# The last but one GRU step's chain in halves of the width, with accumulators of its own for z and for the transposes

## The chip, the cores and the metric

The kernel runs on one core of one Trainium2 chip. A core has TensorE (matrix products[...]), VectorE and ScalarE (elementwise work, both can read PSUM), GpSimd (POOL) and SyncE, which here only starts transfers. The metric is the device time of one execution in microseconds, lower is better.

## The reference

Two layers are computed in float32 on an input x of 128 sequences, 64 steps and a width of 512. The first layer runs a GRU over the steps, projects its states with a ternary weight, and adds the result to x:

```python
def cell(h, x):
    gi = x @ W_ih + b_ih
    gh = h @ W_hh + b_hh
    i_r, i_z, i_n = jnp.split(gi, 3, axis=-1)
    h_r, h_z, h_n = jnp.split(gh, 3, axis=-1)
    r = jax.nn.sigmoid(i_r + h_r)
    z = jax.nn.sigmoid(i_z + h_z)
    n = jnp.tanh(i_n + r * h_n)
    h_new = (1.0 - z) * n + z * h
    return (h_new, h_new)
...
x = x + _L0_ffn_ref(_L0_cond_ref(cond_2048, x, ...), L0_ffn_weight, L0_ffn_bias)
x = x + _L1_ffn_ref(_L1_cond_ref(x, cond_2048[:, None, :], L1_cond_b), ...)
```

The second layer is a causal convolution over the 128 sequences (channel by channel, with `cond_2048` as its taps), and then a mixture of 64 experts of which each token uses 6, with a shared expert beside them. Each GRU step needs the state of the step before; this is what the change is about.

## The kernel before

**Tiles and stages.** The batch of 128 lies on the 128 partitions and the width of 512 along them. The GRU comes first (0 to about 1407 us), then the convolution in 16 slices of the width (to about 1467), then the gating with the first half of the shared expert, then the experts.

**A GRU step.** The loop over `t` (L554) makes, for each of the gates r, n and z in this order, four products of the turned state `hT` with a block of `whh` into an accumulator of 128x512 (`psgh0`, `psgh2`, `psgh1`, L580 to L586). In float32 each product is two records in the profile. VectorE then adds the input part `gi` to r (L590), ScalarE applies the sigmoid (L591); n goes through three VectorE instructions (bias L602, times r L603, plus `gi` L604) and a tanh (L605); z takes one addition (L607) and a sigmoid (L608). The new state is `(h - n) * z + n`, three VectorE instructions (L611, L612, L613). `transposed` (L464) turns it: four 128x128 transposes on TensorE into one accumulator `psf` (`turned_up`, L461), and one copy by ScalarE to `hT` (L467). `parts` (L470) splits `hT` into two pieces, `hhi` and `hlo`, for the projection.

**What lies over the chain.** Inside a step, `ffn(t - 1, ...)` (L478) projects the state of the step before: eight products into `psf` (L490), then VectorE makes `x1` from it (L501), and SyncE stores `x1` twice, once as `x1c` for the convolution (L503) and once to the output (L513). And `stream`, a generator (L430 to L456), gives out the input products of later steps piece by piece (L399, 256 columns wide, into `psx`, `psy`, `psw`, `psz`), ten or eleven pieces a step (L617), so that TensorE has work while VectorE and ScalarE finish a state. The stream has its last pieces in step 61 and none in step 62.

**After the loop.** Three groups of the convolution's first slice go into `psx`, `psy` and `psw` (L626), then the last state's transposes, the fourth group into `psz`, and the last projection. The convolution's slices live in four pairs of buffers, `xc` (inputs, read back from `x1c`) and `tz` (taps); a slice's loads wait until TensorE has finished the slice that used its buffer before. The first two slices' last 16 steps, and slices 2 and 3 whole, are loaded by SyncE right behind the stores of step 61's `x1` (L507 to L511). `psc` rotates over four accumulators; VectorE adds each group to `hid` (L691). `tail_products` (L658) is a little extra work on `xl` and `tap` there.

**What sets the order.** The program is written in one order, and a scheduler reorders the instructions of each engine from it and puts in the semaphores; `tc.issue_after(i)` keeps an instruction behind another one. Each engine works through its own list in order.

## Time and profile before

| what | value |
|---|---|
| median of three runs | 2647.52 us (2647.27, 2647.52, 2649.79) |
| the profiled execution's own time | 2647.67 us |
| its span, first to last instruction | 2645.9 us |
| TensorE busy | 2631.8 us, 99% of the span |
| VectorE, ScalarE, POOL busy | 1402.9, 427.4, 453.2 us |
| TensorE's share of the chain that ended last | 98% |
| granted TensorE clock | 1.00 |

A row of the profile that tells of a group of instructions has the line, the engine, the operation, what it writes and reads, the shape and the count; then the group's busy time, the mean of one in ns, and how long its engine had been idle before it and on whom it waited. A row of the timeline has the start and the length in us first. The chain of waits is followed back from the last instruction, always to what released the one before; "issue" in it is time in which an engine waited for nothing that the profile shows. TensorE's records overlap each other, so that the distance between their starts says more than their length.

### The profile page before, as it was taken

The page shows a single profiled execution, that of the slowest core. Times are in us where ns is not written, and L with a number is a line of the kernel's source. Part 1 is how long each engine was busy: PE and PEld are TensorE (multiplying, and loading weights), DVE is VectorE, ACT ScalarE, POOL GpSimd, SP SyncE. Part 2 cuts the span into 40 slices and gives each one's busy share as a digit, 9 for nine tenths or more (in the row PEclk, how much of TensorE's full clock was granted, in tenths as well). Part 3 has the DMA queues.
Part 4 walks back from the last instruction along what each step waited for, and adds up shares of the span by engine and source line. Part 5 has one row for each costly group of instructions (what it writes and reads, how often), then busy time and mean ns, then how long its engine had stood idle before and what let it go on. Part 6 is the DMA issues. An engine that isn't in the chain of part 4 may idle for free.

```text
span 2645.9 us, 31136 instructions
## 1 busy us (share of the span) xinstructions
PE 2631.8 (99%) x11985; PEld 1823.5 (69%) x11985; DVE 1402.9 (53%) x3103; ACT 427.4 (16%) x791; POOL 453.2 (17%) x516
## 2 busy tenths in 40 slices
PE   9999999999999999999999999999999999999999
PEld 7666666666666666666668767788886666666667
DVE  6555555555555555555557755666674433433344
ACT  1111111111111111111110222222321111111111
POOL 2112111111112121111114100000002222222210
PEclk9999999999999999999999999999999999999999
DMA  5333233232322222322228911222356999998952
GB/s 197 74 58 66 56 60 61 53 61 53 61 47 52 44 52 44 76 44 52 44 60 293 332 41 26 40 66 66 82 148 185 283 313 278 302 326 271 297 174 48
DMA packets 476276, 323.33 MB, mean 122 GB/s; under 512 B 329056, under 2 KB 396512, under 8 KB 473952
## 3 DMA queue, kind: packets, MB, share of 16 engines
q1 hardware_dynamic: 447536, 248.18, 33.7%
q0 software_dynamic: 28592, 73.16, 11.4%
q8 instruction: 95, 1.56, 0.2%
q14 instruction: 53, 0.43, 0.1%
HBM read 235.01 MB, written 92.55 MB: 124 GB/s over the span
## 4 chain that ended last, share of the span: by engine, by line
PE 98%; DVE 1%; DMA 1%; issue 0%; SPq 0%; ACT 0%; DVEq 0%
PE psgh L583 25%; PE psz L787 7%; PE psw L787 7%; PE psx L787 7%; PE psz L399 6%; PE psw L399 6%; PE psx L399 6%; PE psf L490 4%; PE y L787 4%; PE py L1502 3%; PE psy L399 3%; PE pg L1476 3%; PE pu L1476 3%; PE y L962 2%; PE psc L182 2%; PE psf L461 1%
## 5 line engine op out<-in xcount | busy, mean ns | idle before, releaser
L583 PE MATMUL psgh<-whh,hT 128*128 128x512 f32 x1536 | 674.5, 595 | 0.7 <-ACT hT L467 0.7
L583 PEld LDWEIGHTS psgh<-whh,hT 128*128 128x128 f32 x1536 | 286.8, 190 | 350.7 <-issue 336.5
L399 PE MATMUL psx<-wih,xp 128*128 128x256 f32 x744 | 191.0, 379 | 0.0
L220 POOL DMA_DIRECT2D xn<-in_x_dram x61 | 33.8, 555 | 840.6 <-DVE x L501 828.2
L399 PEld LDWEIGHTS psx<-wih,xp 128*128 128x128 f32 x744 | 139.0, 190 | 18.0 <-issue 0.5
L1485 DVE SCALAR_TENSOR_TENSOR a<-a,rw,pu 128x352 f32<-128x352 f32 x32 | 18.6, 580 | 220.3 <-PE pu L1476 220.3
L602 DVE TENSOR_TENSOR n<-psgh,bhn 128x512 f32<-128x512 f32 x64 | 44.2, 691 | 171.0 <-PE psgh L583 171.0
L467 ACT COPY hT<-psf 128x512 f32<-128x512 f32 x64 | 37.5, 587 | 559.0 <-PE psf L461 558.9
L590 DVE TENSOR_TENSOR r<-psgh,gi 128x512 f32<-128x512 f32 x64 | 44.2, 691 | 141.7 <-PE psgh L583 141.7
L1064 POOL DMA_DIRECT2D out_dram<-hid x32 | 27.6, 1000 | 451.8 <-issue 332.9
L486 POOL TENSOR_TENSOR xn<-xn,fb 128x512 f32<-128x512 f32 x61 | 77.0, 1262 | 144.4 <-DMA xn<-in_x_dram 144.4
L399 PE MATMUL psz<-wih,xs 128*128 128x256 f32 x372 | 95.6, 379 | 0.1
L399 PE MATMUL psy<-t,xs 128*128 128x256 f32 x372 | 95.5, 379 | 0.0
L399 PE MATMUL psw<-t,xp 128*128 128x256 f32 x372 | 95.5, 379 | 0.0
L399 PE MATMUL psz<-t,xs 128*128 128x256 f32 x372 | 95.5, 379 | 0.0
L399 PE MATMUL psw<-wih,xp 128*128 128x256 f32 x372 | 95.4, 379 | 0.0
L490 PE MATMUL psf<-sgn,hhi 128*128 128x512 f32 x256 | 94.9, 492 | 0.3 <-DVE hlo L475 0.3
L1502 PE MATMUL py<-wd,aeT 128*64 128x512 f32 (+1 forms) x384 | 89.5, 601 | 0.0
L605 ACT ACTIVATE n<-n 128x512 f32<-128x512 f32 x64 | 40.3, 629 | 277.2 <-DVE n L604 277.2
L414 DVE TENSOR_TENSOR p<-psx,bi 128x512 f32<-128x512 f32 x93 | 64.3, 691 | 36.7 <-PE psx L399 36.7
L787 PE MATMUL psx<-xr,swg 128*128 128x256 f32 x320 | 83.3, 383 | 0.0
L787 PE MATMUL psx<-hid,swg 128*128 128x256 f32 x320 | 82.4, 380 | 0.0
(323 smaller groups left out, 4747.7 us busy)
## 6 DMA issues: line engine op xcount, KB each, us to landing
wg<-in_w_gate_dram SPq DMA_DIRECT2D x64, 704.0 KB
wu<-in_w_up_dram SPq DMA_DIRECT2D x64, 704.0 KB
wd<-in_w_down_dram SPq DMA_DIRECT2D x64, 512.0 KB
x1c<-x SPq DMA_DIRECT2D x62, 256.0 KB
out_dram<-x SPq DMA_DIRECT2D x62, 256.0 KB
xn<-in_x_dram POOLq DMA_DIRECT2D x61, 256.0 KB, 4.1
xp<-in_xT_dram POOLq DMA_DIRECT2D x30, 512.0 KB, 5.7
xc<-x1c SPq DMA_DIRECT2D x28, 512.0 KB
```

Of the source, the lines that this page charges most:

```text
L182: i = nc.tensor.matmul(ps[rows, j].rearrange("p h (u t) -> p h u t", u=2), xcs[sl % NCB][:, rows, g * 4 + j], tzs[sl % NCB][:, :, :, g * 4 ...
L399: i = nc.tensor.matmul(ps, self.ops[n][:, k, :], self.ws[n][:, k, :], start=(first and k == 0), stop=(k == HK - 1), skip_group_check=not f ...
L414: add(self.p1, both, b)
L486: nc.gpsimd.tensor_add(xn, xn, fb)
L490: nc.tensor.matmul(ps, piece[:, k, :], sgn[:, k, :], start=(i == 0 and k == 0), stop=(i == 1 and k == KD - 1),)
L583: nc.tensor.matmul(ps, hT[:, k, :], whh[c][:, k, :], start=(k == 0), stop=(k == KD - 1))
L590: i = nc.vector.tensor_add(r, ps_r, gis.pop((t, 0)))
L602: nc.vector.tensor_add(n, ps_n, bhn)
L787: i = nc.tensor.matmul(ps.rearrange("p (j b) -> p j b", b=P) if len(r.shape) == 3 else ps, lhs(k), r, start=(first and k == 0), stop=(k == ...
L962: nc.tensor.matmul(gu.rearrange("p (j b) -> p j b", b=P), swr[:, k].rearrange("p w n -> p (w n)"), rows[:, k], start=(k == 0), stop=(k == ...
L1476: nc.tensor.matmul(acc[halves[j]], self.xeT[:, k, halves[j]], self.ws[j][which][:, k, :], start=(k == 0), stop=(k == KD - 1),)
L1502: nc.tensor.matmul(py[halves[j]], self.aeT[:n, c, halves[j]], self.ws[j][2][:n, c, :], start=(c == 0), stop=(c == len(ech) - 1),)
```

## The change

In step 62 (`t == T - 2`) and nowhere else the work behind the n gate is done in two halves of 256 columns:

- z's products are made in halves, into two accumulators taken from the pool of the input products, `psx` for the left half and `psy` for the right one.
- The instructions on n, then those on z and on the new state, run once for each half.
- The transposes go into `psw` instead of `psf`, and ScalarE's copy to `hT` becomes two copies.
- `x1` of step 61, which is made in the same step, is ordered behind the last instruction of the new state.

In all other steps the instructions are those of before; the loops have one turn there. Beyond step 62 the scheduler's lists differ in one place: in `tail_products`, the second multiplication on `xl` stands right behind the first, and eight of VectorE's additions to `hid` follow it that stood between the two.

```diff
-        def turned_up(src):
-            ps = ps_f.tile([P, D], F32, name="psf").rearrange("p (k b) -> p k b", k=KD)
+        def turned_up(src, ps=None):
+            if ps is None:
+                ps = ps_f.tile([P, D], F32, name="psf")
+            ps = ps.rearrange("p (k b) -> p k b", k=KD)
...
-        def transposed(src):
-            ps = turned_up(src)
+        def transposed(src, by=1):
+            ps = turned_up(src, ps_gi.tile([P, D], F32, name="psw") if by == 2 else None)
             hT = el0.tile([P, KD, B], F32, name="hT")
-            nc.scalar.copy(hT, ps)
+            for n in range(by):
+                part = slice(n * KD // by, (n + 1) * KD // by)
+                nc.scalar.copy(hT[:, part], ps[:, part])
             return hT
...
-            nc.vector.scalar_tensor_tensor(x1, ps, scale, xn, ALU.mult, ALU.add)
+            with tc.issue_after(summed[-1].ins) if t == T - 3 else nullcontext():
+                nc.vector.scalar_tensor_tensor(x1, ps, scale, xn, ALU.mult, ALU.add)
...
+            by = 2 if t == T - 2 else 1
+            parts_ = [slice(n * D // by, (n + 1) * D // by) for n in range(by)]
             ps_g = []
             for c in (0, 2, 1):
-                ps = ps_gh.tile([P, D], F32, name=f"psgh{c}")
-                for k in range(KD):
-                    nc.tensor.matmul(
-                        ps, hT[:, k, :], whh[c][:, k, :], start=(k == 0), stop=(k == KD - 1)
-                    )
-                ps_g.append(ps)
-            ps_r, ps_n, ps_z = ps_g
+                if c == 1 and by == 2:
+
+                    pss = [ps_gi.tile([P, D], F32, name=f"ps{n}") for n in "xy"]
+                else:
+                    pss = [ps_gh.tile([P, D], F32, name=f"psgh{c}")]
+                for n, ps in enumerate(pss):
+                    piece = parts_[n] if len(pss) == 2 else slice(0, D)
+                    for k in range(KD):
+                        nc.tensor.matmul(
+                            ps[:, piece],
+                            hT[:, k, :],
+                            whh[c][:, k, piece],
+                            start=(k == 0),
+                            stop=(k == KD - 1),
+                        )
+                ps_g.append(pss)
+            (ps_r,), (ps_n,), pss_z = ps_g
...
+            gi_n, gi_z = gis.pop((t, 2)), gis.pop((t, 1))
+            for p in parts_:
+                nc.vector.tensor_add(n[:, p], ps_n[:, p], bhn[:, p])
+                nc.vector.tensor_mul(n[:, p], n[:, p], r[:, p])
+                nc.vector.tensor_add(n[:, p], n[:, p], gi_n[:, p])
+                nc.scalar.activation(n[:, p], n[:, p], AF.Tanh)
+            for p, ps_z in zip(parts_, pss_z):
+                nc.vector.tensor_add(z[:, p], ps_z[:, p], gi_z[:, p])
+                nc.scalar.activation(z[:, p], z[:, p], AF.Sigmoid)
+
+                nc.vector.tensor_sub(h_new[:, p], h[:, p], n[:, p])
+                nc.vector.tensor_mul(h_new[:, p], h_new[:, p], z[:, p])
+                summed.append(nc.vector.tensor_add(h_new[:, p], h_new[:, p], n[:, p]))
...
             if t < T - 1:
-                hT = transposed(h)
+                hT = transposed(h, by)
```

VectorE's list in step 62, from the n gate on, is then: n plus bias, left and right; times r, left and right; plus `gi`, left and right; z left; `h - n` left and right; times z left; z right; plus n left; times z right; plus n right; `x1`. ScalarE's is: tanh left and right, sigmoid left and right, the two copies. In the changed program both copies stand behind the fourth transpose, and the first two products of step 63 wait for the first copy, the next two for the second.

More of the change, by code (lines that the diff above doesn't have):

```diff
@@ L601, in adaln_ffn_kernel @@
             n = el0.tile([P, D], F32, name="n")
-            nc.vector.tensor_add(n, ps_n, bhn)
-            nc.vector.tensor_mul(n, n, r)
-            nc.vector.tensor_add(n, n, gis.pop((t, 2)))
-            nc.scalar.activation(n, n, AF.Tanh)
             z = el0.tile([P, D], F32, name="z")
-            nc.vector.tensor_add(z, ps_z, gis.pop((t, 1)))
-            nc.scalar.activation(z, z, AF.Sigmoid)
             h_new = el0.tile([P, D], F32, name="h")
-            nc.vector.tensor_sub(h_new, h, n)
-            nc.vector.tensor_mul(h_new, h_new, z)
-            nc.vector.tensor_add(h_new, h_new, n)
+            gi_n, gi_z = gis.pop((t, 2)), gis.pop((t, 1))
[10 more added lines that the diff above has]
+                summed.append(nc.vector.tensor_add(h_new[:, p], h_new[:, p], n[:, p]))
             if t > 0:
```

## The prediction

> **What bounds the kernel now.** The page first: TensorE is busy 2631.8 of 2645.9 us and holds 98% of the chain that ended last, so only time in which TensorE stands still, or gets more work, can move the end. Then the table of waits for TensorE alone (who waits for whom: us in total, times, longest). The two largest rows that belong to a GRU step are single events:

> ```profile
> PE psf L461 <- DVE h L613: 1.7, 1, 1.7
> ...
> PE psgh L583 <- ACT hT L467: 0.7, 1, 0.7
> ```

> The transposes of h (L461) waited once, and the products behind them once; in the other 62 steps other products cover that. The chain in order of time (start, us, what) says where:

> ```profile
> 1372.32 6.88 PE psgh L583 x16
> 1379.20 0.02 issue
> 1379.22 0.70 DVE n L602
> ...
> 1383.45 0.64 ACT z L608
> ...
> 1384.73 0.74 DVE x L501
> 1385.47 0.61 DVE h L613
> 1386.08 0.04 issue
> 1386.13 0.67 PE psf L461 x4
> 1386.80 0.02 issue
> 1386.82 0.59 ACT hT L467
> 1387.42 0.04 issue
> 1387.46 10.57 PE psgh L583 x24
> ```

> This is step 62, the only one with a successor but with no input products left to lay over its tail. The reader should see the chain leave TensorE at 1379.20, when the n gate is complete, run through VectorE and ScalarE, and come back at 1386.13. TensorE was not idle all that time: the timeline shows it on z and on the projection of step 61 until 1384.46, and, for comparison, step 61's transposes and copy, which had work beside them:

> ```profile
> 1370.51 0.60 PE L461 MATMUL psf<-ident,h 128*128 128x128 f32 x4
> 1371.14 0.59 ACT L467 COPY hT<-psf 128x512 f32<-128x512 f32 x1 [5.16 <-PE psf L461]
> 1383.38 1.08 PE L490 MATMUL psf<-sgn,hlo 128*128 128x512 f32 x4
> 1385.39 0.68 DVE L613 TENSOR_TENSOR h<-h,n 128x512 f32<-128x512 f32 x1
> ```

> So the hole is 1384.46 to 1386.13 (1.67) and 1386.79 to 1387.46 (0.67): 2.34 us in the whole kernel, and no change here can save more by this road.

> Prices for halves come from groups kept apart by shape (busy, mean ns):

> ```profile
> L426 DVE TENSOR_TENSOR gi<-psw,u 128x256 f32<-128x256 f32 x93 | 39.2, 421 | 27.2 <-PE psw L399 27.2
> L831 ACT ACTIVATE g<-g 128x256 f32<-128x256 f32 x80 | 33.3, 416 | 92.9 <-DVE g L830 91.0 <-DVE rw L1463 1.8
> L816 ACT COPY u<-psx 128x256 f32<-128x256 f32 x80 | 29.7, 371 | 84.1 <-PE psx L787 83.8 <-PE psb L1329 0.3
> ```

> Last, windows of the stage that follows (us, busy by engine, granted clock, DMA share, GB/s):

> ```profile
> 1400.00:1404.00 4.00, 4.00 (x62) 3.71 (x62) 2.08 (x4) 0.56 (x1) 0.55 (x1) 1.00 0.25 98
> 1420.00:1430.00 10.00, 10.00 (x178) 10.00 (x177) 9.08 (x26) 0.00 (x0) 6.31 (x12) 1.00 1.01 336
> ```

> The convolution begins with idle DMA engines and soon fills them: the place where a gain could be lost.

> [...] the trace has 691 and 421, so a half costs 0.61 of a whole. [...] the trace has 416, which I use. [...] in the changed program's semaphores, the first half of the hT copy waits for the fourth transpose, not the second. [...] the trace agrees so far as the copy starts 0.03 us after the last transpose. [...] In the trace step 61's loads for the transposes start at 1370.29, their matmuls at 1370.51.

> **The change part by part.** All times on the clock of the profile before; TensorE is unchanged until 1379.22.

> TensorE: z's four 512-wide products become eight 256-wide ones into psx and psy. A 512-wide product is two records 0.43 us apart: 3.43 us. A 256-wide record is 0.216 us (a row "0.86 PE psw L399 x4" of the chain): 16 x 0.216 = 3.46. Cost +0.03, in the open. Bounds: 0 and +0.3 (weight loads of 0.19 us that stop hiding, which L399 doesn't show). Added waits on TensorE's own semaphore (psy, the next step's psgh2, later psw) are for products at least 5 us old: nothing, at most 0.05 each. The first z half is complete near 1380.95, the second near 1382.7.

> VectorE, in its new order, with starts 0.33 us apart for independent halves, 0.46 for dependent ones (0.42 + 0.04) and 0.06 more for a separate wait: n+b halves 1379.22 and 1379.56; times r 1379.95, 1380.29; plus gi 1380.63, 1380.97; first z add 1381.31; first h-n 1381.65; second h-n after the second tanh. ScalarE: tanh 1381.09 and 1381.50, sigmoid of the first half 1381.94 to 1382.36. Then first h*z 1382.40, second z add 1382.74, first h+n 1383.08 to 1383.50; second sigmoid 1383.20 to 1383.61; second h*z 1383.64; second h+n 1384.10 to 1384.52. Before, h was complete at 1386.07: 1.55 earlier. 0.66 of this (its 0.74 less 0.08 of overlap) comes from x1 (L501), which stood ahead of h+n and is now ordered behind it.

> Transposes: the projection ends at 1384.46 + 0.03 = 1384.49. The first two wait for the first half (1383.50), long there. The third waits for 1384.52 + 0.05, plus a weight load of 0.1 = 1384.68, while TensorE reaches it at 1384.49 + 0.22 = 1384.71. So the 1.67 goes whole, with only 0.03 to spare; the next thing late would be the second half. Behind that waiting transpose stand the other transpose and all of step 63. Bounds on the second half's arrival: 0.2 earlier saves nothing more; 0.1 dearer on each of five handovers costs 0.5.

> Copy: step 61 shows 0.63 from the transposes' start to the copy's. So 1385.13; a half takes 0.37, then 0.05: step 63 starts at 1385.55. The second copy (to 1385.87) hides behind the products of the first two k, 4 x 0.43 = 1.72. Before 1387.46: **gain 1.91 us**.

> x1 of step 61 and its stores: x1 waits for the projection (0.27 behind it before) and for the second h+n: 1384.76 against 1384.73. SyncE's order is untouched: the x1c store, the out store, then the convolution's first loads, which go at +0.03. Those loads were issued from 1390.19 on, and the first slice's landed, by the semaphore records, at 1393.69; its matmuls started at 1399.80 and would now at 1397.89. 4.2 us of cover are left; without it, each us late costs one.

> tail_products: its second multiply on xl (0.68 us) moves eight evictions forward, right behind the first (1.21). The evictions behind then run up to 1.8 us late; four accumulators at 0.92 us a group cover 3.7. Cost nothing; uncovered, at most 0.68. POOL's and SP's lists are the same, in order and waits.

> After that, the slice loads of SP and POOL are each released by TensorE's matmuls of the slice before in that buffer, so DMA demand moves with TensorE; in 1400 to 1404 DMA is 0.25 busy, so there is room for it 1.9 us earlier. The end moves with it. Sum against the profiled execution, 2647.67 (span 2645.9 and 1.8 around it): 2645.76. The median of the three runs is 0.15 below it, so **2645.6**.

> **Rivals.** *The gain is taken by DMA* (2647.0, between 2646.3 and 2647.5). From 1412 the engines are full, and the chain later holds 14.02 us of "DMA swu" from 1461.21. For: share 1.01 and more. Against: what it waits for is issued after TensorE's slices, and DMA's idle room lies before. Chance 0.15. *The second half is late* (2646.1): 0.5 us of the hole stays, at the third transpose. For: 0.03 to spare in a sum of fourteen steps. Against: every duration is a measured one. Chance 0.17. *The chain by halves is longer than by wholes* (slower, 2649.4): one mechanism, in step 62: fourteen VectorE instructions for seven. From the second half on, step 63 follows h by some 0.95 us (load 0.1, two transposes, 0.2 to the copy, 0.37, handovers) instead of 1.39, so it turns at h complete by 1386.51, 2.0 later than my sum, or 0.14 on each of fourteen. If halves cost as much as wholes (0.27 more each, 3.8 us), it is 1.8 slower. Against: 421 ns. Chance 0.03. That it doesn't do what it says: x1 could still stand ahead of h; the changed program's order has it behind.

> **How the numbers follow.** Forecast (gain 1.6 to 2.2) 0.65; the rivals as above. Low end: the hole's whole 2.34 and three runs' scatter downwards (0.25), rounded, 2644.8; high end: no gain, and part of the scatter upwards (one of three runs lay 2.3 above the median), 2648.2. A measurement tells about 0.2%, 5.3 us, from no change; the largest possible gain is under half of it. Faster by more 0.01, within 0.97, slower 0.02.

> **What would show it.** TensorE's wait for h gone or under 0.1, the one for hT about 0.6 to 0.65 from transposes to products; psgh of step 63 at 1385.55; first convolution matmul at 1397.9; everything in the expert stage 1.9 earlier. Wrong if the third transpose waits over 0.3, if TensorE waits for xc, or if the shift has shrunk by 1500.

## The result, and the profile after

| | before | after |
|---|---|---|
| median of 22 executions each, run side by side (us) | 2648.93 | 2645.72 |
| lowest and highest (us) | 2646.78, 2652.87 | 2644.43, 2647.31 |
| the profiled execution, and its span (us) | 2647.67, 2645.9 | 2645.99, 2644.3 |
| first addition of the n gate in step 62 to step 63's first `psgh` product (us) | 1379.22 to 1387.46: 8.24 | 1379.60 to 1385.81: 6.21 |

The ratio of the times is 0.9988 [0.9982, 0.9993]: 3.2 us fewer, between 1.9 and 4.8 by the interval. The two profiled executions don't share a zero of time (the one of after reaches step 62 0.38 us later, before any instruction of the change), so every comparison below is of distances within one execution.

The chain of waits of after in step 62 (start, us, what):

```profile
1379.56 1.73 PE psx L598 x8
1381.29 1.73 PE psy L598 x8
1383.02 1.85 PE psf L494 x8
1384.87 0.48 PE psw L463 x4
1385.36 0.02 issue
1385.38 0.38 ACT hT L471
1385.76 0.04 issue
1385.81 6.28 PE psgh L598 x14
```

The chain no longer leaves TensorE for VectorE and ScalarE at the n gate. It runs through z's products, step 61's projection (`psf`) and the transposes, and leaves TensorE once, for the first half of the copy. The table of who waits for whom, TensorE alone, agrees:

```profile
PE pst L1108 <- DVE hid L1118: 1.3, 1, 1.3
...
PE psw L809 <- DVE u L843: 0.8, 1, 0.8
PE psgh L598 <- ACT hT L471: 0.5, 1, 0.5
```

There is no row any more for transposes that wait for h (1.7 before), and the wait for hT went from 0.7 to 0.5. VectorE's timeline shows why the transposes found h ready (start, us, engine, line; two halves back to back share a row; the bracket is idle time and what ended it):

```profile
1383.39 0.41 DVE L635 TENSOR_TENSOR h<-h,n 128x256 f32<-128x256 f32 x1
1383.96 0.43 DVE L634 TENSOR_TENSOR h<-h,z 128x256 f32<-128x256 f32 x1 [0.15 <-ACT z L631]
1384.42 0.43 DVE L635 TENSOR_TENSOR h<-h,n 128x256 f32<-128x256 f32 x1
1384.96 0.75 DVE L506 SCALAR_TENSOR_TENSOR x<-psf,scale,xn 128x512 f32<-128x512 f32 x1
```

The left half of h is complete at 1383.80, 1.07 us before the first transpose of the chain, and the right half at 1384.85, just as the projection ends (1384.87). x1 runs after both.

To follow the gain to the end of the kernel I use the *lag*: the time behind VectorE's addition for the r gate of step 62, the last event that is alike in all versions. Before, the same addition of step 63 comes 15.41 us behind it; after, 13.38.

| lag of (us) | before | after | lead |
|---|---|---|---|
| r gate, step 63 | 15.41 | 13.38 | 2.03 |
| first convolution product | 24.02 | 21.97 | 2.05 |
| first `psc` product | 32.05 | 30.10 | 1.95 |
| last group of `psc` products | 90.21 | 89.11 | 1.10 |
| router products (`lg`) | 96.34 | 94.75 | 1.59 |
| shared expert, `psz` from swu | 111.81 | 109.82 | 1.99 |
| end of the span | 1270.08 | 1268.12 | 1.96 |

The lead of 2.03 shrinks to 1.10 in the convolution that DMA feeds, and is back at 1.99 in the shared expert. The windows of after there (us, busy by engine in the order TensorE, its weight loads, VectorE, ScalarE, GpSimd, then granted clock, DMA share, GB/s) show the DMA engines busy all the time:

```profile
1412.00:1440.00 28.00, 27.87 (x480) 27.71 (x479) 24.96 (x68) 0.00 (x0) 14.98 (x29) 1.00 1.01 342
1440.00:1460.00 20.00, 18.63 (x302) 17.91 (x301) 15.14 (x43) 0.00 (x0) 8.77 (x17) 1.00 0.99 326
```

So at step 63 the trace shows a gain of about 2.0 us, as forecast, while the medians differ by 3.2. The rows of the table behind the convolution are those of one pair of executions; the repeats below show how much they scatter. The experiments take the chain apart, and look for the missing 1.2.

### The profile page after: what moved, and what is told of

Its sections match the earlier page's. It is cut to its first block, busy times and chain, and to the rows that moved or that the text cites. A ratio compares the mean times of both kernels' runs of the same rounds, so it can differ in the third digit from the quotient of the medians.

```text
span 2644.3 us, 31163 instructions
## 1 busy us (share of the span) xinstructions
PE 2632.3 (100%) x11993; PEld 1825.1 (69%) x11993; DVE 1405.0 (53%) x3110; ACT 427.4 (16%) x794; POOL 453.0 (17%) x516
## 4 chain that ended last, share of the span: by engine, by line
PE 99%; DVE 0%; DMA 0%; issue 0%; ACT 0%; DVEq 0%
PE psgh L598 25%; PE psz L809 7%; PE psw L809 7%; PE psx L809 7%; PE psz L399 6%; PE psw L399 6%; PE psx L399 6%; PE psf L494 4%; PE y L809 4%; PE py L1524 3%; PE psy L399 3%; PE pg L1498 3%; PE pu L1498 3%; PE y L984 2%; PE psc L182 2%; PE lg L1132 1%
## 5 line engine op out<-in xcount | busy, mean ns | idle before, releaser
L399 PE MATMUL psx<-wih,xp 128*128 128x256 f32 x744 | 191.0, 379 | 0.0
L399 PEld LDWEIGHTS psx<-wih,xp 128*128 128x128 f32 x744 | 139.0, 190 | 18.0 <-issue 0.5
L625 DVE TENSOR_TENSOR n<-psgh,bhn 128x512 f32<-128x512 f32 (+1 forms) x65 | 44.3, 683 | 171.3 <-PE psgh L598 171.3
L490 POOL TENSOR_TENSOR xn<-xn,fb 128x512 f32<-128x512 f32 x61 | 77.1, 1263 | 143.8 <-DMA xn<-in_x_dram 143.8
L399 PE MATMUL psz<-wih,xs 128*128 128x256 f32 x372 | 95.6, 379 | 0.1
L399 PE MATMUL psy<-t,xs 128*128 128x256 f32 x372 | 95.5, 379 | 0.0
L399 PE MATMUL psw<-t,xp 128*128 128x256 f32 x372 | 95.5, 379 | 0.0
L399 PE MATMUL psz<-t,xs 128*128 128x256 f32 x372 | 95.5, 379 | 0.0
L399 PE MATMUL psw<-wih,xp 128*128 128x256 f32 x372 | 95.4, 379 | 0.0
L628 ACT ACTIVATE n<-n 128x512 f32<-128x512 f32 (+1 forms) x65 | 40.4, 623 | 276.8 <-DVE n L627 276.8
```

Of the source, the lines that this page charges most:

```text
L399: i = nc.tensor.matmul(ps, self.ops[n][:, k, :], self.ws[n][:, k, :], start=(first and k == 0), stop=(k == HK - 1), skip_group_check=not f ...
L490: nc.gpsimd.tensor_add(xn, xn, fb)
L625: nc.vector.tensor_add(n[:, p], ps_n[:, p], bhn[:, p])
```

## Experiments

All were profiled once; those with 13 or more executions were timed beside the kernel before. `h` below means the state of step 62, and *distance* the time from the first addition of its n gate to step 63's first `psgh` product (8.24 before, 6.21 after). Both kernels are also run again unchanged, to see how much of a reading belongs to the single execution.

### The kernel before, again, and x1's order alone

The first has no edit; the second is the kernel before with one of the change's edits:

```diff
-            nc.vector.scalar_tensor_tensor(x1, ps, scale, xn, ALU.mult, ALU.add)
+            with tc.issue_after(summed[-1].ins) if t == T - 3 else nullcontext():
+                nc.vector.scalar_tensor_tensor(x1, ps, scale, xn, ALU.mult, ALU.add)
...
-            nc.vector.tensor_add(h_new, h_new, n)
+            summed.append(nc.vector.tensor_add(h_new, h_new, n))
```

> The kernel before, unchanged, profiled and timed again. Distance meant in all runs: from the first addition of step 62's n gate on VectorE (n<-psgh) to the first product of step 63 on TensorE (psgh<-whh,hT); 8.24 us in the profile of before, 6.21 in that of after. Theory 'the hole alone' (the change is worth the part of TensorE's hole that it closes, 2.03 us in the profiles, and nothing beside it): distance 8.24 within 0.05, ratio of the times 1.0000 with an interval of about 0.0005 on both sides. Rival 'before is slowed elsewhere as well' (the medians differ by 3.2 us, 1.2 more than the profiles do, so that before must have a wait that its first profile did not show): the time from step 63 to the end comes out over 0.5 us longer than the 1258.4 us of the first profile.

> The kernel before with one thing of the change: x1 of step 61 ordered behind the last instruction of the new state. No halves. The prediction's term: h+n no longer waits for x1, 0.66 us earlier, so the distance is 8.24 - 0.66 = 7.58 and the time 0.7 us under before. Rival 'the stores of x1 matter' (x1 starts 0.6 later, and so do the convolution's first loads): the first convolution product does not come 0.66 earlier, or waits for the loads. The scheduler's list also has the second multiplication of tail_products behind the first here, as in the changed kernel; if that costs anything, TensorE waits for VectorE in the convolution's groups near it, up to 0.68 us.

Before again: 2649.05 (13 executions), ratio 1.0001 [0.9992, 1.0009]. x1's order alone: 2649.69 (13), ratio 1.0001 [0.9993, 1.001]; the expected 0.7 us did not come. Its chain of waits:

```profile
1384.40 0.70 DVE h L613
1385.11 0.02 issue
1385.13 0.04 DVE h L614
...
1385.74 0.76 DVE x L502
1386.49 0.04 issue
1386.54 0.67 PE psf L461 x4
```

h + n (L614) is now ahead of x1 (L502), but the transposes still start only when x1 ends: they are written into `psf`, the accumulator that x1 has yet to read. Moving x1 turns the wait for h into a wait for `psf`: h itself is complete 0.53 us sooner behind the n gate (6.32 against 6.85), but the distance is 8.37 against 8.24.

The repeat of before showed something else. The distance is the same (8.24), but step 63 behind the hole takes longer. The chain:

```profile
1387.64 12.26 PE psgh L583 x24
```

In the first profile the same 24 records take 10.57. The windows of the repeat (columns as above, each engine with the number of its instructions that touch the window):

```profile
1384.43:1387.84 3.41, 1.07 (x6) 0.63 (x6) 1.82 (x3) 0.81 (x2) 0.00 (x0) 1.00 0.30 33
1387.84:1391.25 3.41, 3.41 (x5) 1.33 (x5) 0.69 (x1) 0.39 (x1) 0.00 (x0) 0.50 0.65 125
1391.25:1394.66 3.41, 3.41 (x9) 1.50 (x9) 0.69 (x1) 0.63 (x1) 0.00 (x0) 1.00 0.66 181
```

The clock column reads 0.50 for 3.41 us right behind the hole: five records of products touch that window, nine the next. The lag of step 63 is 17.11 instead of 15.41: **1.70 us lost by the clock, not by the chain**. From step 63's first product to the end the repeat takes 1259.13 us and the first profile 1258.41, 0.72 more, as the rival expected; the other 1.0 of the 1.70 is made up in the stages behind, which differ from execution to execution. x1's order alone has the same stretch (24 records in 12.26 us).

### After, again, and the copy in one piece

```diff
-            for n in range(by):
-                part = slice(n * KD // by, (n + 1) * KD // by)
-                nc.scalar.copy(hT[:, part], ps[:, part])
+            nc.scalar.copy(hT, ps)
```

> The changed kernel, unchanged, profiled and timed again on the chip of the other runs of this set. 'The hole alone': distance 6.21 within 0.05, time 2.0 us under before, ratio 0.9992. Rival 'before is slowed elsewhere as well': ratio 0.9988 or less, 3.2 us. On the convolution: 'DMA eats a part of the lead and gives it back' (in the first profile the lead fell from 2.0 us at its start to 1.1 at its end and was 2.0 again by the shared expert) expects that the same dip is there again; 'scatter of one execution' expects another course.

> The changed kernel with one copy of 512 columns from the turned state to hT in place of two of 256. Theory of the prediction: only the first copy's length is on the path, 0.59 instead of 0.37, so the distance is 6.21 + 0.22 = 6.43. Rival 'the products wait for the second copy anyway': no difference.

After again: 2645.57 (21 executions), ratio 0.9986 [0.998, 0.9993]. The ratio is the one that the expectation gave to a kernel before that is slowed elsewhere as well. The distance is 6.21 and the lag of step 63 13.38, as in the first profile of after, with no low clock behind step 62. The dip in the convolution came again: the last group of `psc` products lies 90.03 behind the r gate, against 90.21 before. There was one later, in the expert stage; TensorE's timeline:

```profile
1471.36 1.25 PE L1108 MATMUL pst<-ident,hid 128*128 128x128 f32 x8 [2.11 <-DVE hid L1118]
1472.55 4.17 PE L1132 MATMUL lg<-hid,gw 128*64 128x256 f32 x16
```

The same row in the first profile of after:

```profile
1469.74 1.25 PE L1108 MATMUL pst<-ident,hid 128*128 128x128 f32 x8 [1.29 <-DVE hid L1118]
1470.92 2.55 PE L1132 MATMUL lg<-hid,gw 128*64 128x256 f32 x16
```

A wait of 2.11 instead of 1.29 us, and the router's products take 4.17 instead of 2.55: clock 0.50 from 1473.05 for 3.41 us. It is a second place where a low clock follows a short stop.

The copy in one piece (one execution): step 63 starts 6.41 behind the n gate, against 6.21; 0.59 for the copy instead of 0.38. The half copy is worth 0.2 us, as expected.

### The banks, one by one

A bank is, in this text, the room of one accumulator of 128x512 (`psx`, `psw`, `psf`) in PSUM, where these kernels have their products and transposes written. That each half needs one of its own rested ahead of these runs on the semaphores of the changed program and was not shown by a trace. Each run takes one bank away from the kernel after, or gives it one more:

```diff
# z_one_bank
-                    pss = [ps_gi.tile([P, D], F32, name=f"ps{n}") for n in "xy"]
+                    pss = [ps_gh.tile([P, D], F32, name="psgh1")] * 2
# transposes_in_psf
-            ps = turned_up(src, ps_gi.tile([P, D], F32, name="psw") if by == 2 else None)
+            ps = turned_up(src)
# transposes_two_banks: each half's two transposes in an accumulator of its own, and its copy
...
+            for n, name in enumerate("wz"):
+                part = slice(n * KD // 2, (n + 1) * KD // 2)
+                ps = ps_gi.tile([P, D], F32, name=f"ps{name}").rearrange("p (k b) -> p k b", k=KD)
+                for k in range(KD)[part]:
+                    nc.tensor.transpose(ps[:, k, :], src[:, k * P : (k + 1) * P], ident)
                 nc.scalar.copy(hT[:, part], ps[:, part])
...
```

> The changed kernel with both halves of z in one accumulator, psgh1. Theory: the left z addition then waits for the last z product of the right half, as the hT copy waits for the fourth transpose; left z at 3.45 us behind the first n addition instead of 2.01, the right half of h complete some 0.6 us later, and the transposes with it: distance 6.7 to 6.8. Rival 'the banks are not what matters, TensorE has the slack': distance 6.21 to 6.3.

> The changed kernel with the transposes in psf, as before, in place of psw. Theory: they wait until x1 has read the projection out of psf, and x1 now stands behind h; x1 ends 6.11 us behind the first n addition, so the transposes start at 6.16 instead of 5.27 and the distance is about 7.1. Rival 'the projection's accumulator is free in time': 6.21.

> The changed kernel with the left two transposes in psw and the right two in psz. Theory: the first copy no longer waits for the third and fourth transposes, and starts 0.25 us earlier: distance 5.95. Rival 'the copy is released later than the bank allows' (for instance by the right half of h): 6.2.

With z's halves in one bank the chain leaves TensorE again, now at the end of z's products:

```profile
1382.16 0.43 DVE z L630
1382.60 0.02 issue
1382.62 0.43 ACT z L631
1383.05 0.03 issue
1383.07 0.76 DVE h L634 x2
1383.83 0.35 DVE h L635
1384.18 0.04 issue
1384.22 0.79 PE psw L463 x4
```

The first z half (L630) starts only at 1382.16, when the second is multiplied too, and h is late. With the transposes in `psf` they wait for x1 instead:

```profile
1384.64 0.76 DVE x L506
1385.40 0.04 issue
1385.45 0.67 PE psf L463 x4
```

And with the two transposed halves in two banks the first copy follows the second transpose, not the fourth:

```profile
1384.30 0.23 PE psw L480 x2
1384.54 0.02 issue
1384.56 0.38 ACT hT L481
```

| version, one execution each | lag of step 63 (us) | against after |
|---|---|---|
| after | 13.38 | |
| copy in one piece | 13.59 | +0.21 |
| z's halves in one bank | 13.92 | +0.54 |
| transposes in `psf` | 14.45 | +1.07 |
| transposes in two banks | 13.12 | -0.26 |

These four expectations held within 0.2 us. Together with x1's order alone they show that the parts of the change aren't a sum: x1 moved without `psw` gains nothing, and with x1 moved `psw` is worth 1.07. `psw` without x1 moved was not run; in the chain of before x1 stands ahead of h + n, so that `psf` is read before h is there, and nothing would wait for it. All of this holds for the programs with their semaphores; what the chip would do without them was not tested.

### The first half's transposes between the two halves of the projection

The hole of 0.46 us that after has left is the half copy and its handovers. In this version the left half of h is transposed between the projection's two groups of four products (`hhi`, `hlo`), in `psw`, and the right half behind them, in `psz`:

```diff
+        def turned_half(src, hT, n, behind_):
+            part = slice(n * KD // 2, (n + 1) * KD // 2)
+            ps = ps_gi.tile([P, D], F32, name="ps" + "wz"[n]).rearrange("p (k b) -> p k b", k=KD)
+            with tc.issue_after(behind_.ins):
+                for k in range(KD)[part]:
+                    i = nc.tensor.transpose(ps[:, k, :], src[:, k * P : (k + 1) * P], ident)
+            nc.scalar.copy(hT[:, part], ps[:, part])
+            return i
...
+                if between and i == 0:
+                    turned = between(mm)
...
```

> The left two transposes (into psw) stand between the two pieces of the projection, the right two (into psz) behind it. Theory: the left half of h is complete 4.2 us behind the first n addition, the first piece of the projection ends at 4.35, so the left transposes cost no wait, their copy ends under the second piece, and step 63 follows the right transposes without any hole: distance 3.42 + 1.85 + 0.48 = 5.75, which is all that was left (0.46), time 2.5 us under before, ratio 0.9990 by the hole alone. Rival 'something else holds step 63' (the left half late, or the copy behind the second sigmoid): 5.9 to 6.2.

The chain shows TensorE without a gap from step 62 to step 63:

```profile
1382.69 0.93 PE psf L504 x4
1383.62 0.36 PE psw L478 x2
1383.98 0.93 PE psf L504 x4
1384.91 0.22 PE psz L478 x2
1385.13 6.87 PE psgh L611 x16
```

2645.57 (20 executions), ratio 0.9985 [0.9978, 0.9991]. The lag of step 63 is 12.76: 0.62 less than after, 2.65 less than before.

### Is it the clock? The hole filled, and the versions side by side

If the missing 1.2 us are the clock's, then the kernel before must gain them when TensorE is kept busy in the hole without the chain becoming shorter. Three 256-wide products are added behind step 61's projection; their results are never read, and nothing of the computation is left out:

```diff
...
+            if t == T - 2:
+                fill = ps_gi.tile([P, D], F32, name="psx")
+                for _ in range(3):
+                    with tc.issue_after(last_mm[-1].ins):
+                        last_mm.append(
+                            nc.tensor.matmul(fill[:, :HD], hT[:, 0, :], whh[0][:, 0, :HD], start=True, stop=True)
+                        )
```

The fourth run of this group does the same for the wait in the expert stage: the version of the section above with four unread 128-wide products ahead of the second `pst` group (again nothing is left out):

```diff
+        fill = ps_l.tile([P, 2, 2, P], F32, name="lg")
+        for _ in range(4):
+            nc.tensor.matmul(fill[:, 0, 0], ident, ident, start=True, stop=True)
         for t in (NB, NB + 1):
             second[t], last = turn(t)
```

> The kernel before with three products of 256 columns more, whose result nobody reads, between step 62's projection and its transposes: 1.3 us of TensorE work laid into the hole of 1.67. The chain is that of before. Clock theory (in a share of its executions the hole lowers TensorE's granted clock to one half for 3.41 us, as the second profile of before shows behind step 62, which costs 1.7; so the change saves 2.0 by the shorter hole and 1.2 to 1.6 on average by a clock that stays up): distance still 8.24 within 0.1, granted clock 1.00 behind it, and time 1.2 to 1.6 us under before, ratio 0.9994 to 0.9995. Rival 'the hole's own length and nothing else': distance 8.24 and ratio 1.0000.

> The changed kernel a third time, on the chip of this set, to set beside early_half_again and filled_hole. Clock theory: 3.2 to 3.6 us under before (ratio 0.9986 to 0.9988), so some 2 under filled_hole. Rival 'hole alone': 2.0 under before and 2.0 under filled_hole.

> The version with the left transposes between the pieces of the projection again, beside the changed kernel on one chip. By the profiles step 63 follows 0.6 us earlier than in the changed kernel: 0.3 to 0.6 us under after_third. Rival: what is won at step 63 is given back where the convolution is fed by DMA, so no difference.

> The same with four products of 128 columns that nobody reads, 0.9 us, in TensorE's wait for the turned first rows behind the convolution (0.9 to 2.5 us in the profiles). Clock theory: the half clock that three of ten profiles show there, at 1473 us, does not appear; 0.3 to 0.5 us under early_half_again on average and a smaller scatter. Rival 'the four products are only more work': the same or up to 0.5 us longer.

The filled hole in TensorE's timeline (the three products show as L630):

```profile
1384.49 1.46 PE L630 MATMUL psx<-whh,hT 128*128 128x256 f32 x6
1386.30 0.66 PE L462 MATMUL psf<-ident,h 128*128 128x128 f32 x4 [0.36 <-DVE h L616]
1387.63 0.70 PE L586 MATMUL psgh<-whh,hT 128*128 128x512 f32 x1 [0.68 <-ACT hT L468]
```

The distance is 8.24, the lag 15.41, to the hundredth those of before, so the chain is no shorter. The times: 2647.71 (13 executions) against 2649.02 for before on the same chip (63), ratio 0.9996 [0.9988, 1.0004]. 1.3 us is what the clock theory expected, but the interval of the ratio includes 1. The kernel after, on the same chip, lies 2.03 us under it (2645.68), which is what its chain is shorter by. The granted clock decides, since it is listed for every execution, as a mean over the span to three digits: one stretch of 3.41 us at half clock is 1.7 of 2646 us and shows as 0.999.

| version | executions | mean clock 0.999 | mean time of these | mean time at 1.000 |
|---|---|---|---|---|
| before (three groups of runs) | 141 | 81 | 2650.14 | 2648.25 |
| x1's order alone | 13 | 6 | 2650.67 | 2648.74 |
| the hole filled | 13 | 1 | 2647.22 | 2648.01 |
| after (three groups) | 64 | 5 | 2647.03 | 2645.75 |
| first half early (two groups) | 41 | 4 | 2645.86 | 2645.47 |
| first half early, wait filled | 19 | 2 | 2645.51 | 2644.98 |

Before has a lowered clock in 81 of 141 executions, and those take 1.89 us longer (95%: 1.5 to 2.2). With the hole filled it is 1 of 13, where before on the same chip has 35 of 63; at full clock the two differ by 0.29 us (-0.4 to 1.0), which is nothing that can be told. A few 0.999 remain in every version. They need not be a drop inside the kernel: the profiles of the copy in one piece and of the early half, again, list 0.999 with a low clock in the last 2.8 us of the span only.

On the chip of these four runs: after 2645.68 (21), ratio 0.9985 [0.9978, 0.9992]; first half early 2645.36 (21), 0.9986 [0.998, 0.9993]; with the wait filled 2645.05 (19), 0.9983 [0.9976, 0.999]. With the fill TensorE waited 0.43 at the second `pst` group. Whether that spares the clock there can't be told: 0.999 is listed in 2 of 19 executions, and without the fill in 1 of 21. The three lie in the order of their profiles, but 0.3 us apart with overlapping intervals: the 0.62 us at step 63 are seen in the trace, and the times don't separate these versions. The last is the shortest measured; that it beats the kernel after is likely, not shown.

## Why the prediction was right, and what it missed

**The mechanism: as forecast.** The hole closed, and for the reasons given. From the n gate, h was complete after 5.25 us (forecast 5.30) and the projection ended after 5.27 (forecast 5.27). z's products took 1.73 + 1.73 = 3.46, as priced, the added waits on TensorE's own semaphore with them, the half copy 0.38 for 0.37. The third transpose didn't wait: h was complete 0.02 us ahead of the projection's end, and by the prediction's own reckoning (0.15 from h to the third transpose, 0.22 from the projection's end) 0.09 was to spare, not 0.03. The rival "the second half is late" is out, narrowly. "The chain by halves is longer" is out as well: halves cost 0.41 to 0.43. The prediction's 691 and 421 ns are a 128x512 and a 128x256 TENSOR_TENSOR in the trace of before, and its 416 ns a 128x256 ACTIVATE.

**A term mis-sized: the copy's start.** The prediction had "step 61 shows 0.63 from the transposes' start to the copy's", and added it to the end of the projection. The copy came 0.51 behind that end. The 0.63 was counted from the start of the transposes' record, and TensorE's records overlap: in after that record starts at 1384.71, and the projection's ends at 1384.88. A time from a start was added to an end. The gain at step 63 is 2.03 instead of 1.91, and TensorE's wait for hT 0.5 instead of 0.6 to 0.65.

**A true sum with a wrong share.** "0.66 of this comes from x1" holds only with the transposes in `psw`: alone, the order brings h forward by 0.53 and step 63 by nothing. The sum was right since both edits are in the change, but as a price of one edit the 0.66 was wrong: the prediction did not ask which accumulator x1 holds while it is late.

**The rival that DMA takes the gain** had its place right, and the first pair of profiles makes it look more clearly refuted than it is. In that pair 0.95 of the lead is gone by the end of the convolution, the waits behind it are shorter by as much (the table of waits: `pst` for hid 1.8 before and 1.3 after, `psw` for u 1.2 and 0.8), and at the end of the span 1.96 is left. The loss comes again: from the first to the last `psc` product the four executions whose chain is no shorter than before's (the first profile, the repeat, x1's order alone, the hole filled) take 57.4 to 58.2 us, the ten with a shortened chain 58.8 to 60.9. The return does not: the repeat of before has 1.0 and 0.8 in the same two waits, no more than after. The end of the span lies 1268.12 behind step 62 in the first profile of after, 1268.64 in the third, and 1268.88 with the hole filled, against 1270.08 before, though the clock was full in all four. What speaks against the rival are the times: at full clock after is 2.64 us faster on the last chip and 2.41 (95%: 1.9 to 2.9) on the one of the first repeats, neither under the 2.03 of step 63. Where the convolution's loss is made up stays open, and that DMA causes it was not tested. `tail_products`, priced at nothing, cost nothing: in the first profile of after its second instruction on `xl` (an addition, not a second multiplication) starts at 1416.07, and TensorE's next wait in the convolution ends at 1440.82.

**What was missed: the clock behind the hole.** The prediction said "the hole's whole 2.34" is the most that can be gained. In the executions timed side by side on the last chip the mean gain is 2649.31 - 2645.75 = 3.56. It splits by the listed clock: executions at 1.000 alone differ by 2.64 (2.1 to 3.1); before has 35 of 63 at 0.999, each 1.81 longer, which adds 1.01; after's 1 of 21 takes back 0.09. The claim about the largest gain left that out. What is left at full clock, 2.64, lies 0.6 above the 2.03 that step 63 shows, which is just outside its interval; on the other chip (2.41) the interval takes it in. If the rest is real, it lies in the stages behind, which differ between profiles by as much.

**The predicted time was met partly by two errors that cancel.** 2645.6 was the median of the three executions first shown (2647.52) less 1.91. The median of 22 lies 1.41 higher, and the gain is larger than forecast by 1.3, so that 2645.72 lies so close to it by luck. What the forecast earned is the 1.91 against 2.03 at step 63. Two of the three had 2647.3 and 2647.5, the third 2649.79. The range took the third for scatter; by the table above, two groups some 1.9 us apart are what before does. The three come without a clock, so this stays a reading.

## What to carry to other kernels

A stop of TensorE can cost more than its length (1.70 us of lowered clock behind the 1.67 in the repeat of before): look at the granted clock of several executions where TensorE stops for as long as here (1.7 to 2.5 us ahead of the drops), since the one profile at hand may be of an execution that was spared, and unread products in the stop show what the clock takes. An instruction moved off the critical path frees it only if nothing on the path needs what the moved one still reads (8.37 us with x1 moved alone, 8.24 without); splitting a chain in halves paid in full only with an accumulator for each half on both sides, as the banks taken away one by one showed (0.54 us lost for z, 1.07 for the transposes, 0.26 still to be had). Where records overlap, count a duration from the event to which it will be added. And before a difference in a late stage is put down to a change, look whether a repeat of the unchanged kernel has it too.

## What was unexpected of the hardware

```profile
1382.37:1385.78 3.41, 2.09 (x9) 1.31 (x7) 2.71 (x5) 0.63 (x1) 0.00 (x0) 1.00 0.08 24
1385.78:1389.19 3.41, 2.38 (x8) 1.29 (x9) 0.98 (x2) 1.20 (x2) 0.00 (x0) 1.00 0.66 70
```

In the repeat the whole hole fell into one window, with 1.07 us busy (the first row of the windows shown there), and the clock fell. I laid each execution's own grid over both places, 1378 to 1392 and 1455 to 1485, in all fourteen profiles. TensorE was busy for 1.70 us or less in six of the grid's windows: 0.88, 1.07, 1.30, 1.51, 1.62 and 1.70. A half-clock stretch follows five of these, all but the 1.62 (before, 1467.71). It follows none of the windows with 2.07 or more. So the busy time of a window goes with the drops in these runs, but for the one exception, and the length of one gap does not: the same wait of 1.67 us was followed by a drop in the repeat of before and by none in its first profile. My reading is that the phase of the grid decides which executions of one kernel are hit; what the clock follows the traces don't show. An estimate from the first profile of before, with the 1.70 us above as the bound: slid over all phases, a window of 3.41 us at the hole has no more work than that in 49% of them; in the profiles of the filled hole and of after, in none. That fits 81 of 141 for before, some of which can come from elsewhere as in the other versions, and 1 of 13 for the filled hole. No run placed the grid on purpose, so its part was only observed, and one exception is left.
